# Three small edits in a four-layer graph network on one core: two seed copies, small vector instructions, the last store

## The chip, the cores and the metric

The kernel runs on one core of a Trainium2 chip. A core has a matrix engine (PE, with its weight loads shown as PEld), a vector engine (DVE), an activation engine (ACT), a general engine (POOL) and a queue engine (SP); each takes its instructions in order. Matrix products land in PSUM, which has eight banks. Data moves between the main memory and the on-chip memory by 16 DMA engines; transfers are started by instructions in the queue of SP or POOL. The metric is the device time of one execution in microseconds (us), lower is better.

## The reference

The input is a feature matrix x of 3327 x 128 and a sparse symmetric weight matrix adj of 3327 x 3327. Each of four layers adds to x a function of h = relu(layernorm(x)):

```python
# layer 0: attention; 128 "heads" of width 8, the scores of all share adj twice as a bias
a = softmax(einsum('dnh,dmh->dnm', q, k) * 128 ** -0.5 + adj + adj, axis=2)
x = x + einsum('dnm,dmh->dnh', a, v).reshape(n, h * d) @ Wo.T
# layer 1: hyperbolic: h_mul(x, W) = exp_map(log_map(x) @ W), h_add = Moebius addition
h1 = h_add(h_mul(h, embed), embed_bias)
neigh = exp_map_zero(adj @ log_map_zero(h1))
x = x + h_add(h_mul(concatenate((h, neigh), axis=1), layer), layer_bias)
# layer 2: hyperbolic again, with projections into a ball, and relu between two maps
# layer 3: x + (adj / deg) @ h @ W_in + (adj.T / deg_T) @ h @ W_out
```

The maps of the hyperbolic layers scale each row by a number made of norms, tanh and artanh. All is float32.

## The kernel before, in words

**Order.** A first part (L313 to L423) projects q, k and v and writes them to main memory, in halves that PE can take in a faster form. An upper bound for the scores is worked out so that no maximum is needed. Then comes the attention loop (L512 to L747), then the output projection of layer 0 (L804 to L838), then layers 1, 2 and 3 (from L969 on). An older, slower form of the attention stands behind a branch and does not run here.

**The attention loop.** The 3327 query columns are cut into 7 chunks of 476 (the last one 472). The 128 heads are taken four at a time (32 groups, g), and the 3328 keys as 13 pairs of 128-row tiles (q). A unit u is one (chunk, group, pair): 7 x 32 x 13 = 2912 units. For a unit there are two rows of work, r = 0 and 1, each with its own PSUM bank in one of three buffers S[u % 3]. S[0] has three banks, of which a unit uses bank 1 and one of the others in turn (`banks`, L595); S[1] and S[2] have two.

The work of one unit: DVE seeds each of the two banks with a tile of adj, less the bound (`seed`, L620, copy in L623). For each of the four heads j, PE adds a product that turns the scores of head j - 1 into those of head j (`scores`, L625, L629), and ACT takes the exponential of both banks in one instruction into tile e (`exps`, L636, L641). For j = 3 in S[1] and S[2] the exponential is split into two halves, one for each bank, so that the first bank comes free earlier. Then PE multiplies the exponentials of all four heads by the values into one bank po (`values`, L644, L649). After 13 pairs DVE copies po away (L661) and POOL stores it (L665).

The order of the instructions is written out by hand: the loop at L723 runs over slots i, four for a unit, and lists at each slot which unit's exponential, seed, scores and values come next. For u % 3 = 0 the two seeds stand in two different slots (at = 0 and 2). For the others both stand at slot at = 1, one directly after the other. Between slots, DVE also transposes squares of adj for a later chunk (L275, L279).

**Waits.** A framework puts a semaphore wait wherever two instructions touch the same tile. Banks of one tile count as the same tile. `touch` (L606) therefore keeps, for each of the three buffers, the last twelve accesses, and tells the framework of pairs on other banks that they need not wait; of accesses to the same bank it adds the wait by hand. Before the change it does so only for instructions of two different engines, so the second seed of a pair waits, on DVE, for the first.

**The layers.** Rows of x lie as 128 partitions x 26 tiles (row = 26 p + t, so partition 127 holds 25 rows), in the tile xs. A number for each row is a 128 x 26 tile; the class `Small` (L137) has helpers for such tiles, each of which issues one instruction of 26 columns on DVE, or on ACT for a function: `tt` (L147, record at L149), `ts` (L158, L161 and L163), `recip` (L166), `act` (L174, L176), and made of these `sqrt` (L179, ACT's root with one refining step) and `artanh` (L185). `artanh` works out both a series for small arguments and a logarithm for the others and picks by a mask. `ball_sum` (L965) and `sum_norm` (L975) work out the two factors of a Moebius sum and its norm. In this part the framework's scheduler, and not the program's order, places the instructions.

The root is called 16 times (once in the first part, once at L784, once in each of three layer norms, six times in layer 1, five times in layer 2), artanh six times, `ball_sum` three times and `sum_norm` twice. In each layer `aggregate` (L930) loads 26 strips of adj or its transpose, by turns on POOL and SP, and PE multiplies them (L941); DVE sums the strips of some layers (L944).

**The end.** After the last aggregation, seven chunks of four row tiles each (the last has two) are projected (L1095), added into xs by DVE (L928), and stored: partitions 0 to 126 by SP (L1113) and partition 127, which has one row fewer, by POOL (L1115). Where the strips have 127 rows the helper `pieces` (L68) cuts them into 112 and 15.

Of the kernel before, what the change touches and what calls it, by code (L numbers as in the profile page):

```python
# [9 lines left out]

F32 = mybir.dt.float32


# [3 lines left out]
AF = mybir.ActivationFunctionType  # L17
ALU = mybir.AluOpType
# [4 lines left out]
P = 128  # L23
# [4 lines left out]
NT = 26  # L28
# [39 lines left out]
def pieces(m):  # L68

    return [(0, 112), (112, m)] if m == P - 1 else [(0, m)]  # L70
# [13 lines left out]
def gnn_kernel(ctx: ExitStack, tc: tile.TileContext, x, adj, Wq, Wk, Wv, Wo, embed, layer,  # L84
               embed_bias, layer_bias, weight, bias, W_in, W_out, out):
    nc = tc.nc
    dram = ctx.enter_context(tc.tile_pool(name="dram", bufs=1, space=DRAM))
    const = ctx.enter_context(tc.tile_pool(name="const", bufs=1))

    ident = const.tile([P, P], F32, name="ident")  # L90
    make_identity(nc, ident)

    adjT = dram.tile([NP, NP], F32, name="adjT")
    by_tile = adjT.rearrange("(p t) n -> t p n", t=NT)
    v_d = dram.tile([NP, HD], F32, name="v_d")
    n2_d = {s: dram.tile([GP], F32, name=f"n2{s}_d") for s in "qk"}
    kraw_d = dram.tile([H, GP], F32, name="kraw_d")

    qS_d = dram.tile([2, H, GP], F32, name="qS_d")
    kS_d = dram.tile([2, H, HEADS, NP], F32, name="kS_d")  # L100
# [36 lines left out]
    class Small:  # L137
# [33 lines left out]
        def div(self, a, b):  # L171
            return self.mul(a, self.recip(b))

        def act(self, a, f):  # L174
            o = self.new()
            nc.scalar.activation(o, a, f)  # L176
            return o

        def sqrt(self, a):  # L179

            v = self.ts(a, 1e-30, ALU.max)
            s = self.act(v, AF.Sqrt)
            return self.ts(self.add(s, self.div(v, s)), 0.5, ALU.mult)

        def artanh(self, a, top):  # L185

            v = self.ts(a, top, ALU.min)
            v2 = self.mul(v, v)
            s = self.ts(v2, 1.0 / 13.0, ALU.mult, 1.0 / 11.0, ALU.add)
            for k in (9.0, 7.0, 5.0, 3.0, 1.0):  # L190
                s = self.ts(self.mul(s, v2), 1.0 / k, ALU.add)
            s = self.mul(s, v)
            r = self.div(self.ts(v, 1.0, ALU.add), self.ts(v, -1.0, ALU.mult, 1.0, ALU.add))
            g = self.ts(self.act(r, AF.Ln), 0.5, ALU.mult)
            small = self.ts(v, 0.25, ALU.is_lt)
            return self.add(g, self.mul(small, self.tt(s, g, ALU.subtract)))

    def sumsq(sm, a, tmp):
        nc.scalar.activation(tmp, a, AF.Square)
# [113 lines left out]
    with tc.tile_pool(name="a1", bufs=1) as a1, tc.tile_pool(name="a2", bufs=2) as a2, \  # L313
# [3 lines left out]
        xs = load_x(a1)  # L317
# [19 lines left out]
        for t0 in range(0, NT, 2):  # L337
            for s in "kq":
                st = {i: a2.tile([P, H, 2 * P], F32R if s == "q" else F32, name=f"st_{s}{i}")
                      for i in range(2 if s == "q" else 1)}  # L340
                n2 = a2.tile([P, 2, P], F32, name=f"n2{s}")
                for i in range(2):
                    t = t0 + i
# [83 lines left out]
    with tc.tile_pool(name="d1", bufs=1) as d1, tc.tile_pool(name="d2", bufs=2) as d2, \  # L427
# [17 lines left out]
        with tc.If(loose > 0):  # L445
# [28 lines left out]
            for c in range(NC):  # L474
# [5 lines left out]
                with tc.For_i(0, HEADS, 1) as d:  # L480
# [12 lines left out]
                    for t in range(NT):  # L493
                        m = rows_of(t)
                        s = d_ps.tile([P, 4 * P], F32, name="ps_y")
# [16 lines left out]
    with tc.tile_pool(name="e1", bufs=1) as e1, tc.tile_pool(name="e_adj", bufs=30) as e_adj, \  # L512
# [7 lines left out]
        VA = [e1.tile([P, NT, 4, H + 1], F32, name=f"VA{i}") for i in range(2)]  # L520

        seen = e1.tile([P, 3], F32, name="seen")
        S = [e_ps.tile([P, 3 if i == 0 else 2, 512], F32, name=f"S{i}") for i in range(3)]
        po = e_ps.tile([P, 512], F32, name="po")

# [54 lines left out]
        with tc.If(loose < 1), tc.manual_schedule():  # L580
# [25 lines left out]
            def touch(u, rows, x):  # L606
                of = {banks(u)[r] for r in rows}
                for y, other in touched[u % 3]:
                    if not of & other and x.ins.engine != y.ins.engine:
                        tc.declare_no_dep(x.ins, y.ins, reason="other banks")  # L610
                for i in of:
                    if (u % 3, i) in last:
                        tc.add_manual_dep(x.ins, last[u % 3, i].ins.name, after, reason="the same bank")
                    last[u % 3, i] = x
                touched[u % 3].append((x, of))

            def bank(u, r):
                return S[u % 3][:, banks(u)[r], :width_of(pairs[u][0])]

            def seed(u, r):  # L620
                c, g, q = pairs[u]
                w = width_of(c)
                touch(u, [r], nc.vector.tensor_copy(bank(u, r), adj_of[c][2 * q + r][:, :w]))  # L623
# [99 lines left out]
            for i in range(-4, 4 * n + 15):  # L723
                u, j = in_slot(i)
                if 0 <= u < n:
                    exps(u, j)

                u, at = (i + 4) // 4, i % 4
                if u < n and (u % 3 == 0 and at in (0, 2) or u % 3 and at == 1):
                    for r in range(2) if at == 1 else (at // 2,):  # L730
                        seed(u, r)
                u = (i - 14) // 4
                if at == 2 and 0 <= u < n and pairs[u][2] == NQ - 1:
                    store(u)
                if at == 3 and i > 0:
                    for f, a in behind.pop(i // 4, ()):
                        f(*a)
                if at % 2:
                    for k in (1, 2):
                        u, j = in_slot(i + k)  # L740
                        if 0 <= u < n:
                            scores(u, j)
                    u, r = ((i - 11) // 4, 0) if at == 3 else ((i - 13) // 4, 1)
                    if 0 <= u < n:
                        values(u, r)
                if at == 0 and 0 <= i // 4 < n:
                    loads(i // 4)  # L747


    xs = load_x(const)  # L750
# [28 lines left out]
    eb2, lb2, b2 = row_sum("eb2", eb), row_sum("lb2", lb), row_sum("b2", hb)  # L779
    with tc.tile_pool(name="w0", bufs=1) as w0:  # L780
        sm = Small(w0, "s")
# [183 lines left out]
    def ball_sum(sm, coef, aa, ab, y2, least):  # L965

        xy = sm.mul(coef, ab)
        x2 = sm.mul(sm.mul(coef, coef), aa)
        e = sm.ts(xy, 2.0, ALU.mult, 1.0, ALU.add)  # L969
        na = sm.ts(e, y2[:, 0:1], ALU.add)  # L970
        den = sm.ts(sm.add(e, sm.ts(x2, y2[:, 0:1], ALU.mult)), least, ALU.max)
        rd = sm.recip(den)
        return sm.mul(sm.mul(na, coef), rd), sm.mul(sm.ts(x2, -1.0, ALU.mult, 1.0, ALU.add), rd)

    def sum_norm(sm, al, be, aa, ab, y2):  # L975

        b2 = sm.ts(sm.mul(be, be), y2[:, 0:1], ALU.mult)
        n2 = sm.add(sm.mul(sm.mul(al, al), aa), b2)
        return sm.sqrt(sm.add(n2, sm.mul(sm.ts(sm.mul(al, be), 2.0, ALU.mult), ab)))


    with tc.tile_pool(name="g1", bufs=1) as g1:
        sm = Small(g1, "s")
# [5 lines left out]
        a, aa = arr("a", D + 1), sm.new()  # L989
# [9 lines left out]
        ab = a[:, :, D]  # L999
        al, be = ball_sum(sm, c1, aa, ab, eb2, L1_EPS)  # L1000
        yn = sm.ts(sum_norm(sm, al, be, aa, ab, eb2), L1_EPS, ALU.max)
        f = sm.div(sm.artanh(yn, L1_MAX_TANH), yn)
        al, be = sm.mul(al, f), sm.mul(be, f)
        y = arr("y")
# [25 lines left out]
        al, be = ball_sum(sm, c2, ww, w1[:, :, D], lb2, L1_EPS)  # L1030
# [5 lines left out]
    with tc.tile_pool(name="h1", bufs=1) as h1:  # L1036
        sm = Small(h1, "s")
# [3 lines left out]
        a, aa = arr("a", D + 1), sm.new()  # L1041
# [4 lines left out]
        ab = a[:, :, D]  # L1046
        al, be = ball_sum(sm, c1, aa, ab, hb2, L2_MIN_NORM)
# [3 lines left out]
        f = sm.mul(sm.div(sm.artanh(pn, L2_MAX_TANH), pn), pf)  # L1051
        al, be = sm.mul(al, f), sm.mul(be, f)
        y = arr("y")
# [6 lines left out]
        u, rr = arr("y"), sm.new()  # L1060
        for c in range(7):
            ts = tiles_of(c)
# [9 lines left out]
        n2 = sm.ts(sm.mul(t1, p2), L2_MIN_NORM, ALU.max)  # L1072
# [8 lines left out]
    with tc.tile_pool(name="i1", bufs=1) as i1:  # L1081
        sm = Small(i1, "s")
        h = arr("h")
        layer_norm(sm, xs, h)
        deg = sm.new()
        nc.vector.memset(deg, 1.0)

        def over_degree(g):
            pos = sm.ts(g, 0.0, ALU.is_gt)
            return sm.recip(sm.add(sm.mul(g, pos), sm.ts(pos, -1.0, ALU.mult, 1.0, ALU.add)))  # L1090

        def add_projected(c, ps, lhsT, w, r):
            ts = tiles_of(c)
            for t in ts:
                nc.tensor.matmul(ps[:, (t - ts[0]) * P:(t - ts[0] + 1) * P], lhsT[:, t * P:(t + 1) * P], w,  # L1095
                                 start=True, stop=True)
            for t in ts:
                add_scaled(xs[:, t, :], ps[:, (t - ts[0]) * P:(t - ts[0] + 1) * P], r[:, t:t + 1], xs[:, t, :])

        r_out = over_degree(degT)  # L1100
        pu, width = aggregate(h, strip_rows, deg)
        vT = matT("hT")
        by_tiles(pu, width, vT)
        r_in = over_degree(deg)
        pu, width = aggregate(h, strip_T, also={
            3 * c + 4: lambda c=c: add_projected(c, bank_u(7), vT, w_out, r_out) for c in range(7)})
        uT = matT("uT")
        by_tiles(pu, width, uT)
        for c in range(7):
            add_projected(c, next_bank(), uT, w_in, r_in)  # L1110
            ts = tiles_of(c)
            m = ts[-1] + 1 if ts[-1] < NT - 1 else NT - 1
            nc.sync.dma_start(out[0:(P - 1) * NT].rearrange("(p t) d -> p t d", t=NT)[:, ts[0]:ts[-1] + 1, :],  # L1113
                              xs[0:P - 1, ts[0]:ts[-1] + 1, :])
            nc.gpsimd.dma_start(out[(P - 1) * NT + ts[0]:(P - 1) * NT + m].rearrange("(p t) d -> p t d", p=1),  # L1115
                                xs[P - 1:P, ts[0]:m, :])

# [29 lines left out]
```

## Time and profile before

| what | value |
|---|---|
| runs | 11603.74 us median of 3 (11602.49 to 11605.68) |
| the profiled execution, its own time | 11601.16 us |
| its span, first to last instruction | 11599.4 us |
| busy in the span | PE 95%, ACT 90%, DVE 41%, PEld 30%, POOL 16% |
| mean granted PE clock | 0.976 |
| attention loop, first to last exponential | 456.2 to 10572.3 us |
| layers 1 to 3 with the last stores | about 10680 to 11599 us |

The profile is one execution taken by the hardware profiler. For each group of instructions it gives the source line, the engine, the operation, the tiles as out<-in with their shapes, how often it ran, the busy time in all, the mean length of one in ns, and the time that the engine stood idle just before them with what ended most of it. The records of ACT and DVE run from the start of an instruction to the end of its writes, and those of neighbours overlap. The chain that ended last follows the work back from the last instruction to what released it. A helper's line (L149, L161, L928) stands for all that call it.

### The profile page before, as it was taken

Reading aid. Unit: us, or ns where it says so; the run is one execution under the profiler, and the core shown is the slowest. Engines: PE = TensorE matmul, PEld = TensorE weight load, DVE = VectorE, ACT = ScalarE, POOL = GpSimd, SP = SyncE. Lnnn points to the kernel's source line nnn. Section 1 sums busy time; section 2 is a strip of 40 time slices with the busy share of each in tenths; the row PEclk is TensorE's granted clock in tenths of the full one; section 3 lists DMA queues with packets and bytes.
Section 4 is the critical chain, followed back from the end, with each engine's and each line's share of the span. In section 5 each row is a group of like instructions: output and inputs, shape, how many; then the busy total and the mean of one; then the engine's idle time right before and its main releaser. Section 6 shows DMA issues by size and latency. Waiting matters only on the chain.

```text
span 11599.4 us, 196522 instructions
## 1 busy us (share of the span) xinstructions
PE 10982.6 (95%) x72980; PEld 3500.4 (30%) x72980; DVE 4766.2 (41%) x7583; ACT 10411.4 (90%) x14091; POOL 1895.5 (16%) x3254
## 2 busy tenths in 40 slices
PE   4699999999999999999999999999999999998787
PEld 2122222222222222222222222222222222224443
DVE  5344444444444443444444444444443333335631
ACT  3699999999999999999999999999999999995210
POOL 5211112111121111211112111121111211110000
PEclk8799999999999999999999999999999999998888
DMA  8755455554555554555555545555454544443465
GB/s 247 245 90 93 86 93 105 90 92 88 94 103 91 91 88 83 102 93 90 89 92 103 93 89 92 90 105 93 87 92 78 103 81 79 82 78 103 153 230 211
DMA packets 652389, 1242.80 MB, mean 107 GB/s; under 512 B 185742, under 2 KB 527766, under 8 KB 634924
## 3 DMA queue, kind: packets, MB, share of 16 engines
q1 hardware_dynamic: 609768, 1100.81, 48.6%
q0 software_dynamic: 41664, 129.31, 3.7%
q8 instruction: 590, 9.67, 0.4%
q14 instruction: 367, 3.01, 0.1%
HBM read 1082.90 MB, written 146.60 MB: 106 GB/s over the span
## 4 chain that ended last, share of the span: by engine, by line
ACT 80%; PE 8%; issue 6%; DVE 2%; DMA 1%; POOL 0%; SPq 0%; DVEq 0%; POOLq 0%; ACTq 0%
ACT e L641 79%; PE pu L941 5%; PE S L629 1%; PE po L649 1%; DVE S L623 0%; PE pu L893 0%; DMA ot<-oT_d 0%; PE ps_y L837 0%; DVE xs L928 0%; PE pu L916 0%; PE pu L904 0%; POOL a L571 0%; DVE s L149 0%; DMA KT<-kS_d 0%; DVE s L944 0%
## 5 line engine op out<-in xcount | busy, mean ns | idle before, releaser
L641 ACT ACTIVATE e<-S 128x952 f32<-128x952 f32 (+3 forms) x13589 | 10107.1, 914 | 9.0 <-PE S L629 7.7
L623 DVE COPY S<-a 128x476 f32<-128x476 f32 (+1 forms) x5824 | 3739.6, 655 | 5991.9 <-ACT e L641 5731.8
L649 PE MATMUL po<-e,VA 128*9 128x476 f32 (+1 forms) x46592 | 5736.9, 564 | 16.1 <-DVE OS L661 3.1
L629 PE MATMUL S<-QS,KT 64*128 64x476 f32 (+1 forms) x23296 | 5077.6, 442 | 112.2 <-DVE S L623 30.0
L629 PEld LDWEIGHTS S<-QS,KT 64*128 64x128 f32 x23296 | 2273.0, 184 | 5383.0 <-DVE S L623 2705.4
L665 POOL DMA_DIRECT2D oT_d<-OS x896 | 470.7, 531 | 5604.3 <-DVE OS L661 5468.5
L649 PEld LDWEIGHTS po<-e,VA 128*9 128x9 f32 x46592 | 691.2, 88 | 1793.5 <-issue 1694.1
L550 POOL TENSOR_SCALAR QS<-QS 32x476 fp32r<-32x476 f32 (+1 forms) x1344 | 784.7, 584 | 1334.2 <-DMA QS<-qS_d 748.0
L123 ACT COPY uT<-pu 128x494 f32<-128x494 f32 (+1 forms) x12 | 6.6, 547 | 428.6 <-PE pu L941 428.6
L560 POOL COPY VA<-VR 128x832 f32<-128x832 f32 x224 | 198.6, 886 | 951.7 <-DMA VR<-v_d 729.6
L941 PE MATMUL pu<-strip,h 128*128 128x494 f32 (+2 forms) x728 | 293.9, 564 | 40.3 <-ACT h L874 40.3
L941 PE MATMUL pu<-strip,y 128*128 128x494 f32 (+2 forms) x728 | 296.8, 570 | 34.4 <-DVE y L928 19.9
L571 POOL TENSOR_TENSOR a<-a,shb 128x476 f32<-128x476 f32 (+1 forms) x182 | 213.3, 1207 | 245.1 <-DMA a<-adjT 221.3
L275 DVE STREAM_TRANSPOSE cols<-rows 128x416 f32<-128x416 f32 x208 | 203.2, 982 | 21.4 <-DMA rows<-in_adj_dram 14.1
L941 PEld LDWEIGHTS pu<-strip,y 128*128 128x128 f32 (+1 forms) x728 | 139.9, 193 | 190.5 <-issue 157.8
L941 PEld LDWEIGHTS pu<-strip,h 128*128 128x128 f32 (+1 forms) x728 | 138.0, 191 | 192.3 <-issue 141.5
L661 DVE COPY OS<-po 128x476 f32<-128x476 f32 (+1 forms) x224 | 145.6, 650 | 53.2 <-PE po L649 47.2
L123 ACT COPY hT<-pu 128x494 f32<-128x494 f32 (+1 forms) x4 | 2.2, 549 | 136.2 <-PE pu L941 136.2
L407 ACT CAST st_k<-st_q 128x1664 fp32r<-128x1664 f32 x16 | 53.7, 3378 | 75.9 <-DMA st_q<-kraw_d 58.0
L939 POOL DMA_DIRECT2D strip<-adjT x39 | 20.9, 535 | 600.7 <-PE pu L941 598.9
L944 DVE TENSOR_REDUCE s<-strip 128x1 f32<-128x3327 f32 (+1 forms) x26 | 93.9, 3616 | 59.7 <-DMA strip<-in_adj_dram 59.7
L944 DVE TENSOR_REDUCE degT<-strip 128x1 f32<-128x3327 f32 (+1 forms) x26 | 94.0, 3616 | 54.0 <-DMA strip<-adjT 54.0
(173 smaller groups left out, 1714.9 us busy)
## 6 DMA issues: line engine op xcount, KB each, us to landing
KT<-kS_d SPq DMA_DIRECT2D x1792, 208.0 KB
KT<-kS_d SPq DMA_DIRECT2D x1792, 104.0 KB
VR<-v_d SPq DMA_DIRECT2D x224, 416.0 KB
strip<-adjT POOLq DMA_DIRECT2D x39, 1663.5 KB, 7.7
strip<-adjT SPq DMA_DIRECT2D x36, 1663.5 KB
QS<-qS_d SPq DMA_DIRECT2D x3072, 14.9 KB
QS<-qS_d SPq DMA_DIRECT2D x1536, 29.8 KB
adjT<-cols SPq DMA_DIRECT2D x26, 1664.0 KB
```

The lines of the kernel that those rows point to most:

```text
L275: nc.vector.transpose(self.cols[:, t0:t0 + NQ, 32 * j:32 * j + 32], self.rows.rearrange("p (x t) -> p t x", t=NT)[:, t0:t0 + NQ, :])
L550: nc.gpsimd.tensor_scalar(QS[b][r0:r0 + 32, j + 1, :w], QS[b][r0:r0 + 32, j, :w].bitcast(F32), -1.0, 0.0, op0=ALU.mult, op1=ALU.add)
L560: nc.gpsimd.tensor_copy(VA[(c * NG + g) % 2][:, :, :, 0:H], v.rearrange("p j (t e) -> p t j e", e=H))
L571: nc.gpsimd.tensor_tensor(a[:, :w], a[:, :w], shift[:, :w], op=ALU.subtract)
L623: touch(u, [r], nc.vector.tensor_copy(bank(u, r), adj_of[c][2 * q + r][:, :w]))
L629: x = nc.tensor.matmul(bank(u, r), KT[b][64 * r:64 * r + 64, max(0, j - 1), q * P:(q + 1) * P], QS[b][64 * r:64 * r + 64, j, :w], start=Fa ...
L641: touch(u, range(a, b), nc.scalar.activation(e[:, a:b, :w], S[u % 3][:, lo + a:lo + b, :w], AF.Exp, scale=2.0))
L649: nc.tensor.matmul(po[32 * j:32 * j + H + 1, :w], VA[k % 2][:, 2 * q + r, j, :], e_of[u, j][:, at, :w], start=(q == 0 and r == 0), stop=(q ...
L661: nc.vector.tensor_copy(o[:, :w], po[:, :w])
L665: nc.gpsimd.dma_start(oT_d[:, d * N + c * CW:d * N + c * CW + w], o[32 * j:32 * j + H + 1, :w])
L941: nc.tensor.matmul(pu[c][:, :w], y[:m, t, :], s[:m, c * AW:c * AW + w], start=(t == 0), stop=(t == NT - 1))
L944: nc.vector.tensor_reduce(deg[:m, t:t + 1], s[:m], axis=AX.X, op=ALU.add)
```

## The change

There are three edits.

1. In `touch`, an access of DVE to S[1] or S[2] is no longer made to wait for an earlier access of DVE to another bank. Between the two seeds of such a unit, DVE now writes a zero into a tile of one element, `apart`.
2. The small tiles use a fused instruction, (a op0 scalar) op1 b, where two stood before. `sqrt` lets ACT take the root of v / 4 and folds the halving into the fused step. `artanh` takes the logarithm ahead of the series, and the series has one fused step for each coefficient instead of two. `ball_sum` and `sum_norm` are regrouped in the same way.
3. The last store cuts partitions 0 to 126 into 112 on SP and 15 on POOL.

```diff
+        def fused(self, a, s, op0, b, op1):
+            o = self.new()
+            nc.vector.scalar_tensor_tensor(o, a, s, b, op0=op0, op1=op1)
+            return o
         def sqrt(self, a):
             v = self.ts(a, 1e-30, ALU.max)
-            s = self.act(v, AF.Sqrt)
-            return self.ts(self.add(s, self.div(v, s)), 0.5, ALU.mult)
+            s = self.act(v, AF.Sqrt, 0.25)
+            return self.fused(self.div(v, s), 0.25, ALU.mult, s, ALU.add)
         def artanh(self, a, top):
             v = self.ts(a, top, ALU.min)
             v2 = self.mul(v, v)
-            s = self.ts(v2, 1.0 / 13.0, ALU.mult, 1.0 / 11.0, ALU.add)
-            for k in (9.0, 7.0, 5.0, 3.0, 1.0):
-                s = self.ts(self.mul(s, v2), 1.0 / k, ALU.add)
-            s = self.mul(s, v)
-            r = self.div(self.ts(v, 1.0, ALU.add), self.ts(v, -1.0, ALU.mult, 1.0, ALU.add))
-            g = self.ts(self.act(r, AF.Ln), 0.5, ALU.mult)
+            r = self.fused(v, 1.0, ALU.add, self.recip(self.ts(v, -1.0, ALU.mult, 1.0, ALU.add)), ALU.mult)
+            g = self.act(r, AF.Ln)
+            s = self.ts(v2, 1.0 / 13.0, ALU.mult)
+            for k in (11.0, 9.0, 7.0, 5.0, 3.0):
+                s = self.fused(s, 1.0 / k, ALU.add, v2, ALU.mult)
+            s = self.fused(s, 1.0, ALU.add, v, ALU.mult)
             small = self.ts(v, 0.25, ALU.is_lt)
-            return self.add(g, self.mul(small, self.tt(s, g, ALU.subtract)))
+            d = self.fused(g, -0.5, ALU.mult, s, ALU.add)
+            return self.fused(g, 0.5, ALU.mult, self.mul(small, d), ALU.add)
...
+        apart = e1.tile([1, 1], F32, name="apart")
...
                 for y, other in touched[u % 3]:
-                    if not of & other and x.ins.engine != y.ins.engine:
+                    if not of & other and (x.ins.engine != y.ins.engine or u % 3 and x.ins.engine == DVE):
                         tc.declare_no_dep(x.ins, y.ins, reason="other banks")
...
                     for r in range(2) if at == 1 else (at // 2,):
                         seed(u, r)
+                        if at == 1 and r == 0:
+                            nc.vector.memset(apart, 0.0)
...
         e = sm.ts(xy, 2.0, ALU.mult, 1.0, ALU.add)
-        na = sm.ts(e, y2[:, 0:1], ALU.add)
-        den = sm.ts(sm.add(e, sm.ts(x2, y2[:, 0:1], ALU.mult)), least, ALU.max)
-        rd = sm.recip(den)
-        return sm.mul(sm.mul(na, coef), rd), sm.mul(sm.ts(x2, -1.0, ALU.mult, 1.0, ALU.add), rd)
+        rd = sm.recip(sm.ts(sm.fused(x2, y2[:, 0:1], ALU.mult, e, ALU.add), least, ALU.max))
+        na = sm.fused(e, y2[:, 0:1], ALU.add, coef, ALU.mult)
+        return sm.mul(na, rd), sm.mul(sm.ts(x2, -1.0, ALU.mult, 1.0, ALU.add), rd)
...
-        b2 = sm.ts(sm.mul(be, be), y2[:, 0:1], ALU.mult)
-        n2 = sm.add(sm.mul(sm.mul(al, al), aa), b2)
-        return sm.sqrt(sm.add(n2, sm.mul(sm.ts(sm.mul(al, be), 2.0, ALU.mult), ab)))
+        b2 = sm.fused(be, y2[:, 0:1], ALU.mult, be, ALU.mult)
+        cross = sm.mul(sm.fused(al, 2.0, ALU.mult, be, ALU.mult), ab)
+        return sm.sqrt(sm.add(sm.mul(sm.mul(al, aa), al), sm.add(b2, cross)))
...
-            nc.sync.dma_start(out[0:(P - 1) * NT].rearrange("(p t) d -> p t d", t=NT)[:, ts[0]:ts[-1] + 1, :],
-                              xs[0:P - 1, ts[0]:ts[-1] + 1, :])
+            for p0, p1 in pieces(P - 1):
+                (nc.gpsimd if p0 else nc.sync).dma_start(
+                    out[p0 * NT:p1 * NT].rearrange("(p t) d -> p t d", t=NT)[:, ts[0]:ts[-1] + 1, :],
+                    xs[p0:p1, ts[0]:ts[-1] + 1, :])
             nc.gpsimd.dma_start(out[(P - 1) * NT + ts[0]:(P - 1) * NT + m].rearrange("(p t) d -> p t d", p=1),
                                 xs[P - 1:P, ts[0]:m, :])
```

More of the change, by code (lines that the diff above doesn't have):

```diff
@@ L9 @@
 from concourse.masks import make_identity
+DVE = mybir.EngineType.DVE
 F32 = mybir.dt.float32
@@ L172, in div, with act @@
             return self.mul(a, self.recip(b))
-        def act(self, a, f):
+        def act(self, a, f, scale=1.0):
             o = self.new()
-            nc.scalar.activation(o, a, f)
+            nc.scalar.activation(o, a, f, scale=scale)
+            return o
+        def fused(self, a, s, op0, b, op1):
+            o = self.new()
+            nc.vector.scalar_tensor_tensor(o, a, s, b, op0=op0, op1=op1)
             return o
```

## The prediction

> **What bounds the kernel now.** I read the share of each engine first, then the chain that ended last, then the groups of the attention loop, then the records inside one stretch of it, and last the tail. From the page of before: the busy shares, the chain, and three groups (busy time, mean ns of one, then the engine's idle time before them).
>
> ```profile
> PE 10982.6 (95%) x72980; PEld 3500.4 (30%) x72980; DVE 4766.2 (41%) x7583; ACT 10411.4 (90%) x14091; POOL 1895.5 (16%) x3254
> ...
> ACT 80%; PE 8%; issue 6%; DVE 2%; DMA 1%; POOL 0%; SPq 0%; DVEq 0%; POOLq 0%; ACTq 0%
> ...
> L641 ACT ACTIVATE e<-S 128x952 f32<-128x952 f32 (+3 forms) x13589 | 10107.1, 914 | 9.0 <-PE S L629 7.7
> L623 DVE COPY S<-a 128x476 f32<-128x476 f32 (+1 forms) x5824 | 3739.6, 655 | 5991.9 <-ACT e L641 5731.8
> L629 PE MATMUL S<-QS,KT 64*128 64x476 f32 (+1 forms) x23296 | 5077.6, 442 | 112.2 <-DVE S L623 30.0
> ```
>
> The exponentials of L641 fill 10107 us of 11599 with 9 us idle before them. But each record (mean 0.914 us) overlaps its neighbour, so a busy ACT might still be a waiting one. I therefore took starts and ends of single records. In the stretch from 5016 us, ends lie 0.855 to 0.859 us apart for a 952-column tile and 0.460 for a 476-column one, whatever the starts do: one start came 0.942 after the one before it instead of the usual 0.845, and its end came 0.855 after. Over the loop the median distance of ends is 0.857 (8320 tiles of 952), 0.460 (3328 of 476), 0.850 (1387 of 944) and 0.457 (554 of 472). The product is 7130 + 1531 + 1179 + 253 = 10093 us; from first start to last end the loop takes 10116. **ACT is the limit, and only some 23 us of the loop are not its own work.** In 227 places the ends lie more than 20 ns too far apart, 26 us in sum (a few other distances are shorter than the median): this is all that a faster feed can win there.
>
> Second, the end. The timeline of the tail (start, length, engine, what):
>
> ```profile
> 11528.14 6.81 DVE L928 SCALAR_TENSOR_TENSOR xs<-pu,s,xs 128x128 f32<-128x128 f32 x26 [1.25 <-PE pu L1095]
> 11529.29 55.20 SPq L1113 DMA_DIRECT2D out_dram<-xs  x7
> 11529.56 0.52 POOL L1115 DMA_DIRECT2D out_dram<-xs  x1 [30.93 <-DVE xs L928]
> ...
> 11534.72 0.98 POOL L1115 DMA_DIRECT2D out_dram<-xs  x2 [0.55 <-DVE xs L928]
> ```
>
> Compute is over at 11535, yet SP issues stores until 11584.5 and the span ends at 11599.4. The view by stretches sets this beside a stretch in which a 112-row strip piece arrives (the last two columns: share of 16 DMA engines, GB/s):
>
> ```profile
> 11504.00:11510.00 6.00, 6.00 (x19) 3.10 (x18) 0.55 (x2) 0.00 (x0) 0.00 (x0) 1.00 0.94 251
> 11535.00:11598.00 63.00, 0.00 (x0) 0.00 (x0) 0.00 (x0) 0.00 (x0) 0.69 (x2) 0.50 0.07 25
> ```
>
> A share of 0.07 of 16 is about one engine. The 127-row store goes through a single one at 25 GB/s; the 112 + 15 rows of the last strip used 0.94 of all.
>
> **The change, part by part.** *The store* (L1113). 762 packets of 2 KB (median 84 ns) and 127 of 1 KB (46 ns) are now drained one after another. With 112 rows over 16 engines a chunk is 7 packets in a row, 7 x 0.084 = 0.6 us, less than the 1.03 us in which DVE makes a chunk, so SP no longer backs up. What is late next is POOL: it issues 14 stores instead of 7, each 0.49 us (the "0.98 x2" row), so 0.98 per chunk against 1.03: it just keeps up. After DVE's end at 11534.95 come 0.3 us to the first issue, two issues (1.0), landing 4.6 to 5.9 us counted from the start of the last issue, so 11535.7 + 5.9 = 11541.6, and 1.15 us of closing steps (from SP's last store wait at 11598.25 to the end): 11543. Bounds: 11541 with the short landing and nothing queued, 11549 if POOL's issues take twice as long and a 15-row piece sits on one engine (15 x 0.084 = 1.3 us). **Term: 11599.4 - 11543 = -56.4** (-50 to -58).
>
> *The two seeds of a pair* (L623, for u % 3 in 1, 2). Two rows of the loop, starts and lengths:
>
> ```profile
> 5006.41 1.42 DVE L623 COPY S<-a 128x476 f32<-128x476 f32 x2 [1.48 <-ACT e L641]
> ...
> 5009.90 1.97 DVE L623 COPY S<-a 128x476 f32<-128x476 f32 x3 [1.16 <-ACT e L641]
> ```
>
> A pair takes 1.42, so the second starts 0.76 after the first. The third of three, which has no wait on DVE, adds only 0.55. In the records, 752 copies without a wait follow a copy by 0.566, and 24 whose wait on POOL was already met do so too, so a met wait costs nothing. The self-wait goes (0.76 - 0.566 = 0.194), the 1x1 memset comes in; the nearest row is a memset of 128x1, after which DVE starts its next instruction 0.08 later:
>
> ```profile
> 10699.52 0.06 DVE L952 MEMSET uT<- 128x1 f32 x1
> 10699.60 0.29 DVE L869 BATCH_NORM_STATS2 st<-xs 128x6 f32<-128x128 f32 x1
> ```
>
> So the second copy comes 0.194 - 0.08 = 0.114 us earlier. Its own wait for the second half of the exponential is met by then: the half ends 0.46 after the first half, the copy starts 0.65 after the first copy. PE, which waits for it, gains the same; DVE, at 41%, hides 1941 memsets x 0.08 = 155 us. ACT gains only where it ran dry. Taking at most 0.114 off each of the 227 places gives 17 us. In 53 of them (2.8 us) the second copy is seen to be the last event; in most of the others PE is late behind a pair and a row of waits for loads, so it would be earlier too, but not everywhere by all of it. **Term: -12** (0 to -20).
>
> By the Trainium skill, "VectorE: DVE Perf Modes", section "The DRAIN you can't avoid", eight copies take as long with a semaphore after each as with one at the end. By that this term would be 0. The 0.76 against 0.566 above disagrees; the rule stays as a rival.
>
> *Small instructions.* A square root loses one DVE instruction, artanh 7 (23 to 16), the ball sum 2 (13 to 11), the norm of a sum 2 beside its root: 16 + 42 + 6 + 4 = 68. Their worth depends on what stands beside them. A chain in which each needs the one before costs 0.217 a step, as here in the series of artanh:
>
> ```profile
> 10754.06 0.19 DVE L149 TENSOR_TENSOR s<-s,s 128x26 f32<-128x26 f32 x1
> 10754.28 0.18 DVE L161 TENSOR_SCALAR s<-s 128x26 f32<-128x26 f32 x1
> 10754.49 0.19 DVE L149 TENSOR_TENSOR s<-s,s 128x26 f32<-128x26 f32 x1
> 10754.71 0.18 DVE L161 TENSOR_SCALAR s<-s 128x26 f32<-128x26 f32 x1
> ```
>
> With independent work between, a step costs 0.09. Exposed series (PE waits behind them, 10751 to 10758, 11001 to 11005, 11012 to 11017, 11190 to 11196): 4 x 5 steps x 0.217 = 4.3. Two more artanh lie in stretches where DVE is full: 2 x 7 x 0.09 = 1.3. Nine exposed roots: 2.0. Five sums, 2 each at about 0.15: 1.5. Against it stands the fused form: at 128x128 its rows show 0.344 against 0.284 for a plain product, so it may cost up to 0.06 more; at 26 columns I take a fifth of it on 40 exposed ones, 0.5. The earlier logarithm buys little, since its table load is already beside the series. Sum -8.6. Bounds: -4 (fused form at full price, 2.4, and half of the interleaved steps hidden) to -15, because ahead of the last layer four 3.6 us sums of strips stand within the chain of the norm, and one step less may move one of them out or in. **Term: -8.6.**
>
> **Sum.** -56.4 - 12 - 8.6 = -77. The profiled execution took 11601.16 (span 11599.4), 2.6 below the median 11603.74. From 11601.2 that is 11524; with half of the distance to the median, **11526**.
>
> **The rivals.**
> 1. *The self-wait is free, or nothing that ACT waits for hangs on it.* For: 26 us in all, 2.8 seen directly. Against: 0.76 to 0.566. Then -56.4 - 8.6: 11536. Chance 0.20.
> 2. *The starts are ACT's true pace.* Starts lie 0.845 apart at best, and twice in three tiles' turn (10.41 us) one comes later, 0.942 and 0.884: 0.136 us x 970 turns = 132 us would be won, 11404. Against: the even ends. Chance 0.05.
> 3. *The store stays at one engine's speed* (two queues in place of one, same engines). Then only -20.6: 11581. Against: 0.94 of the engines at 112 rows. Chance 0.05. The Trainium skill, "DMA: Bandwidth & Descriptors", section "Rules for kernel authors", says that spreading DMAs over issuing engines gives no bandwidth; by that alone this case would hold, were the row count not changed as well.
> 4. *Slower: the memset is no filler but a second link.* If it waits for the first copy and the second copy for it, the spacing becomes 0.76 + 0.06 + 0.10 = 0.92, 0.16 later than now. In the stretch read, ACT has 0.04 us in hand after a late pair (records of 1.00 against 0.964 where it ran dry), so 0.12 is lost per pair: 1941 x 0.12 = 233 us, 11769. It decides from a spacing of 0.80 on and eats the other terms at 0.80 + 65/1941 = 0.833. Against: the memset writes a tile that no copy touches. Chance 0.06.
>
> **How the numbers follow.** Forecast 0.64 (11526), rivals 0.20, 0.05, 0.05, 0.06. The range takes the forecast with its bounds and the first rival: low 11526 - 20, high 11536 + 8: 11506 to 11544. Rivals 2 to 4 and a little of the others lie outside. A measurement tells 0.2% (23 us) from no change: faster 0.89 (forecast, rivals 1 and 2), same 0.05 (rival 3), slower 0.06.
>
> **What would show it.** Store: SP's seven issues within 8 us instead of 55, the span's end within 9 us of the last DVE instruction. Pair: two copies with the memset in 1.30 us instead of 1.42, ends of the exponentials still 0.857 apart, L641's total unchanged, L629's idle and the 227 places fewer. Layers: 68 DVE instructions fewer beside 1941 memsets, series at five steps. It would be wrong if ends move closer than 0.857 (rival 2), the pair grows beyond 1.46 (rival 4), or SP still issues long after DVE is done.

## The result and the profile after

The changed kernel takes 11513.02 us (median of 4 runs, 11505.02 to 11513.99) against 11603.58 (4 runs) for the kernel before in the same comparison: a ratio of 0.992, 95% interval 0.9903 to 0.9937. The profiled execution took 11513.99 us, its span is 11512.2. Between the two spans lie 87.2 us.

The page of the kernel after: busy shares, the chain that ended last, and the same groups as before (lines have moved: L650 is the exponential, L632 the seed, L638 the scores).

```profile
PE 11042.9 (96%) x72980; PEld 3752.1 (33%) x72980; DVE 4640.8 (40%) x9456; ACT 10396.0 (90%) x14091; POOL 1895.0 (16%) x3261
...
ACT e L650 59%; PE po L658 13%; PE S L638 12%; PE pu L952 5%; PE pu L904 0%; PE ps_y L848 0%; PE pu L927 0%; DVE OS L670 0%; DVE xs L939 0%; DMA ot<-oT_d 0%; PE pu L915 0%; DVE s L955 0%; DMA KT<-kS_d 0%; PE ps_t L844 0%; DVE s L935 0%
...
L650 ACT ACTIVATE e<-S 128x952 f32<-128x952 f32 (+3 forms) x13589 | 10091.6, 1067 | 4.0 <-PE S L638 3.7
L632 DVE COPY S<-a 128x476 f32<-128x476 f32 (+1 forms) x5824 | 3620.0, 660 | 6100.6 <-ACT e L650 6052.3
L638 PE MATMUL S<-QS,KT 64*128 64x476 f32 (+1 forms) x23296 | 5147.0, 446 | 24.9 <-DVE S L632 20.2
```

PE's idle time before the scores fell from 112.2 us to 24.9; 30.0 and 20.2 of these are put down to a seed, in 42 and 3 waits. The exponential's mean record grew from 0.914 to 1.067 us although its total fell: the record begins earlier, with the scores lying ready, and its end still lies 0.857 after the one before. So a longer record here means less waiting. DVE has 1873 instructions more: 1941 memsets less 68.

Both spans, divided at the same events, show where the 87.2 us went:

| stretch (us) | before | after | difference |
|---|---|---|---|
| start to first exponential | 456.2 | 456.8 | +0.5 |
| attention loop | 10116.0 | 10095.6 | -20.4 |
| loop's end to the first aggregation | 185.8 | 183.8 | -2.0 |
| between aggregations, after layer 1's and after layer 2's | 111.1 + 61.7 | 107.1 + 60.3 | -5.4 |
| the aggregations of layers 1, 2 and 3 | 148.4 + 148.4 + 298.5 | 148.2 + 146.9 + 298.4 | -1.8 |
| from the last aggregation product to the end (the tail) | 73.2 | 15.1 | -58.1 |

Layer 3 has two aggregations, one behind the other without a gap. In the loop the median distances of the exponentials' ends are the same as before (857, 460, 850, 457 ns). Places where they lie over 20 ns too far apart (late places) fell from 227 (25.9 us) to 14 (5.3 us).

The timeline of DVE in the loop after (start, length, engine, what):

```profile
5017.43 1.26 DVE L632 COPY S<-a 128x476 f32<-128x476 f32 x2 [2.37 <-ACT e L650]
5018.07 0.06 DVE L742 MEMSET apart<- 1x1 f32 x1
```

A pair takes 1.26 us instead of 1.42. Its ends lie 0.599 apart (median) instead of 0.760.

The tail after, and the view by stretches of its last 12 us (the last two columns: share of 16 DMA engines, GB/s):

```profile
11499.09 6.81 DVE L939 SCALAR_TENSOR_TENSOR xs<-pu,s,xs 128x128 f32<-128x128 f32 x26 [1.25 <-PE pu L1105]
11500.25 6.00 SPq L1124 DMA_DIRECT2D out_dram<-xs  x7
11500.51 0.53 POOL L1124 DMA_DIRECT2D out_dram<-xs  x1 [30.93 <-DVE xs L939]
11501.03 0.53 POOL L1127 DMA_DIRECT2D out_dram<-xs  x1
...
11507.44 0.50 POOL L1127 DMA_DIRECT2D out_dram<-xs  x1
```

```profile
11500.00:11506.00 6.00, 3.97 (x36) 3.77 (x34) 5.90 (x23) 0.00 (x0) 5.18 (x11) 1.00 0.59 181
11506.00:11512.00 6.00, 0.00 (x0) 0.00 (x0) 0.00 (x0) 0.00 (x0) 1.94 (x4) 0.53 0.34 107
```

SP issues its seven stores in 6.0 us, in step with DVE. The DMA engines are 0.59 busy while DVE still works; before, 0.08 then and 0.07 after it had ended. The span ends 6.3 us after DVE's last instruction.

### The profile page after: what moved, and what is told of

It is laid out like the page before. It is cut to its first block, busy times and chain, and to the rows that moved or that the text cites. A ratio compares the mean times of both kernels' runs of the same rounds, so it can differ in the third digit from the quotient of the medians.

```text
span 11512.2 us, 196520 instructions
## 1 busy us (share of the span) xinstructions
PE 11042.9 (96%) x72980; PEld 3752.1 (33%) x72980; DVE 4640.8 (40%) x9456; ACT 10396.0 (90%) x14091; POOL 1895.0 (16%) x3261
## 4 chain that ended last, share of the span: by engine, by line
ACT 59%; PE 31%; issue 4%; DVE 1%; DMA 0%; POOL 0%; SPq 0%; POOLq 0%; DVEq 0%; ACTq 0%
ACT e L650 59%; PE po L658 13%; PE S L638 12%; PE pu L952 5%; PE pu L904 0%; PE ps_y L848 0%; PE pu L927 0%; DVE OS L670 0%; DVE xs L939 0%; DMA ot<-oT_d 0%; PE pu L915 0%; DVE s L955 0%; DMA KT<-kS_d 0%; PE ps_t L844 0%; DVE s L935 0%
## 5 line engine op out<-in xcount | busy, mean ns | idle before, releaser
L650 ACT ACTIVATE e<-S 128x952 f32<-128x952 f32 (+3 forms) x13589 | 10091.6, 1067 | 4.0 <-PE S L638 3.7
L632 DVE COPY S<-a 128x476 f32<-128x476 f32 (+1 forms) x5824 | 3620.0, 660 | 6100.6 <-ACT e L650 6052.3
L658 PE MATMUL po<-e,VA 128*9 128x476 f32 (+1 forms) x46592 | 5737.2, 564 | 15.7 <-DVE OS L670 4.3
L638 PE MATMUL S<-QS,KT 64*128 64x476 f32 (+1 forms) x23296 | 5147.0, 446 | 24.9 <-DVE S L632 20.2
L638 PEld LDWEIGHTS S<-QS,KT 64*128 64x128 f32 x23296 | 2530.0, 183 | 5254.9 <-ACT e L650 2390.7
L340 PE MATMUL ps_t<-wk,hT 128*128 128x512 f32 x104 | 58.8, 700 | 60.8 <-ACT sq L362 60.8
## 6 DMA issues: line engine op xcount, KB each, us to landing
QS<-qS_d SPq DMA_DIRECT2D x1536, 29.8 KB
```

The lines of the kernel that those rows point to most:

```text
L638: x = nc.tensor.matmul(bank(u, r), KT[b][64 * r:64 * r + 64, max(0, j - 1), q * P:(q + 1) * P], QS[b][64 * r:64 * r + 64, j, :w], start=Fa ...
L650: touch(u, range(a, b), nc.scalar.activation(e[:, a:b, :w], S[u % 3][:, lo + a:lo + b, :w], AF.Exp, scale=2.0))
L658: nc.tensor.matmul(po[32 * j:32 * j + H + 1, :w], VA[k % 2][:, 2 * q + r, j, :], e_of[u, j][:, at, :w], start=(q == 0 and r == 0), stop=(q ...
```

## The experiments

Ten kernels. The three single edits and the store with both pieces on SP ran beside one median of the kernel before (11607.7), the cuts at 126 and 113 rows beside another (11599.7), the other four beside a third (11599.8); ratios are against these.

**One edit alone.** Three kernels, each the kernel before with one part of the change.

*The pair alone*:

```diff
-                    if not of & other and x.ins.engine != y.ins.engine:
+                    if not of & other and (x.ins.engine != y.ins.engine or u % 3 and x.ins.engine == DVE):
...
+                        if at == 1 and r == 0:
+                            nc.vector.memset(apart, 0.0)
```

> The kernel before with the first edit alone: no wait between the two seeds of a pair, the memset between them. Theory (ACT is the limit of the attention loop and can win only where it ran dry; in the trace of the changed kernel such places fell from 227 to 14): the loop from first start to last end goes from 10116 to 10096 us, distances of the exponentials' ends stay at 0.857 and 0.460, and the time goes from 11603.6 to 11583. Rival (the loop's 20 us come from elsewhere, a wait on DVE costs nothing): 11603. Rival (the pair is worth more by itself, the other edits hide some of it): below 11575.

Measured: 11587.3, ratio 0.9982 (0.9973 to 0.9991), 20.4 us. The pair's ends lie 0.598 apart, 12 late places are left of the 227; tail and gaps are those of before. The loop took 10103.2 in this execution, 7.6 more than in the kernel after, and no wait accounts for it: the distances of full tiles (952 columns) average 857.7 ns instead of 857.1, all shifted together. So ACT's own pace differs between executions whose loops hold the same instructions; why, no run here shows.

*The store alone*:

```diff
-            nc.sync.dma_start(out[0:(P - 1) * NT].rearrange("(p t) d -> p t d", t=NT)[:, ts[0]:ts[-1] + 1, :],
-                              xs[0:P - 1, ts[0]:ts[-1] + 1, :])
+            for p0, p1 in pieces(P - 1):
+                (nc.gpsimd if p0 else nc.sync).dma_start(
...
```

> The kernel before with the last edit alone: the store of partitions 0 to 126 cut into 112 on SP and 15 on POOL. Theory (the 127-row store used one DMA engine, and this is all that the tail waited for): 58 us less, 11545.5; the end of the span comes 15 us after the last product of an aggregation instead of 73. Rival (part of the shorter tail is due to the shorter chains before it): more than 11550.

Measured: 11548.17, ratio 0.9949 (0.9935 to 0.9962), 59.5 us. Tail 15.5 instead of 73.2; the loop (10115.4, 227 places) is untouched.

*The small instructions alone* (the helpers, `ball_sum` and `sum_norm` as in the change; its core):

```diff
-            for k in (9.0, 7.0, 5.0, 3.0, 1.0):
-                s = self.ts(self.mul(s, v2), 1.0 / k, ALU.add)
+            for k in (11.0, 9.0, 7.0, 5.0, 3.0):
+                s = self.fused(s, 1.0 / k, ALU.add, v2, ALU.mult)
```

> The kernel before with the second edit alone: fewer small instructions. Theory (worth what stands between the aggregations, taken from the two traces: 2.0 + 4.0 + 1.4 us between them and 1.7 us in them): 9 us less, 11594.5. Rival (the instructions were hidden, and the gaps got shorter because the strips came earlier): no change, 11603. The three edits alone should add up to the 87 us between the two traces; if they do not, they help or hinder one another.

Measured: 11597.62, ratio 0.9991 (0.9982 to 1.0), 10.1 us, by the runs alone not told from no change. Its profile shows where it lies: the gaps take 182.9, 108.4 and 60.3 (7.0 less than before), two aggregations 146.9 and 147.3 (2.6 less); loop (10116.0, 227 places) and tail (73.2) as before. Aggregations between 146.9 and 148.5 come up in kernels that share these instructions too, so the 2.6 are not surely the edit's.

The three medians add up to 20.4 + 59.5 + 10.1 = 90.0; all together gave 90.6 (11603.58 - 11513.02). Each edit changed its own stretch of the profile alone, so they do not touch one another. The intervals, 10 us or more to each side, are far wider than the 0.6 between the two sums; that these agree so closely is luck.

**Why the store was slow.** The prediction said: 127 rows go through one DMA engine, 112 and 15 are shared out. Four kernels ask which of it matters: the rows, the second queue, or the queue that issues.

*Both pieces on SP*:

```diff
-                (nc.gpsimd if p0 else nc.sync).dma_start(
+                nc.sync.dma_start(
```

> The changed kernel with both pieces of the store, 112 and 15 rows, on SP's queue. Theory (the row count matters, not the second queue): the end stays within 2 us of the changed kernel's 15 us after the last aggregation, 11511 to 11514; it may come 1 us earlier since POOL has seven stores fewer. Rival (the second queue is what made the tail short): SP backs up again and the end comes 10 us or more later, above 11523.

Measured: 11518.92, ratio 0.9923 (0.9909 to 0.9936). The tail takes 14.7, no longer than with two queues; the 6 us against the kernel after lie mostly in the loop (10102.6, 9 late places, full tiles at 857.6 ns), ACT's pace again. The kernel before, too, was 4.1 us slower beside this run than beside the kernel after. The second queue is worth nothing here.

*127 rows whole, but on POOL*:

```diff
-            for p0, p1 in pieces(P - 1):
-                (nc.gpsimd if p0 else nc.sync).dma_start(
...
+            nc.gpsimd.dma_start(out[0:(P - 1) * NT].rearrange("(p t) d -> p t d", t=NT)[:, ts[0]:ts[-1] + 1, :],
+                              xs[0:P - 1, ts[0]:ts[-1] + 1, :])
```

> The kernel after, but the 127-row store of a chunk stays whole and is issued by POOL instead of SP. Theory (the row count decides: 127 rows have no even share over 16 engines, so they go through one at 25 GB/s, whatever queue issues them): the tail is as long as before, 73 us after the last aggregation product instead of 15, so about 11513 + 58 = 11571 (11560 to 11580). Rival (what cost the 58 us is SP's way of issuing, or its being behind with the strips, and POOL cuts transfers otherwise): tail 15 to 20 us, 11513 to 11520.

Measured: 11510.81, ratio 0.9923 (0.9907 to 0.994), tail 15.2. My theory fell, the rival held. The DMA view of the last stretch and the view by stretches:

```profile
out_dram<-xs POOLq DMA_DIRECT2D x6, 254.0 KB, 3.2
```

```profile
11502.00:11508.00 6.00, 2.00 (x18) 1.81 (x17) 3.93 (x16) 0.00 (x0) 5.77 (x12) 0.89 0.78 226
```

A whole 254 KB store lands 3.2 us after its issue, and the engines are 0.78 busy at 226 GB/s. In the list of packets the same rows stand as 409 of 4 KB and a few odd sizes, where SP's queue had 762 of 2 KB and 127 of 1 KB. So the queue that issues decides too: POOL's shares out 127 rows, SP's does not.

*The cut elsewhere: 126 + 1 and 113 + 14*:

```diff
-            for p0, p1 in pieces(P - 1):
+            for p0, p1 in ((0, 126), (126, P - 1)):
```

> The kernel after, with the 127 rows of a chunk's store cut into 126 on SP and 1 on POOL. Theory (SP's queue shares the rows of a transfer among as many engines as divide the row count, up to 16: 127 rows went to 1, 112 to 16, 15 to 15): 126 rows go to 14 engines, a chunk drains in 9 x 4 packets of 0.084 us, about 3 us at worst, tail 15 to 20 us, 11513 to 11520. Rival (only a multiple of 16 rows is shared out): 126 rows through one engine, tail about 72 us, 11570.

Measured: 11514.69, ratio 0.9926 (0.9909 to 0.9943), tail 15.7.

```diff
-            for p0, p1 in pieces(P - 1):
+            for p0, p1 in ((0, 113), (113, P - 1)):
```

> The kernel after, with the cut one row further: 113 on SP and 14 on POOL. Theory (the divisor of the row count decides, and 113 is a prime): 678 packets of 2 KB and 113 of 1 KB one after another, 678 x 0.084 + 113 x 0.046 = 62 us instead of the 70 of 127 rows, tail 73 - 8 = 65, 11563 (11555 to 11570). Rival (two pieces are enough, or SP's rest beyond 112 goes to another engine): tail 15 to 25, 11513 to 11523.

Measured: 11562.92, ratio 0.9968 (0.9956 to 0.9981), tail 66.6 where 65 was worked out. SP's seven issues, one after another, and the stretch after DVE's end:

```profile
11497.05 48.84 SPq L1124 DMA_DIRECT2D out_dram<-xs  x7
```

```profile
11506.00:11550.00 44.00, 0.00 (x0) 0.00 (x0) 0.00 (x0) 0.00 (x0) 1.20 (x3) 0.50 0.07 27
```

48.84 us and a share of 0.07: the picture of before, with one row more than 112. Two pieces alone do not help, and 126 rows, no multiple of 16, do. The trace agrees with a count of engines: on SP's queue each engine that takes part in a transfer closes it with a packet of 4 bytes, and for seven stores there are 7 of these with 127 rows, 112 with 112, 105 with 15, 98 with 126, and 7 with 113, so 1, 16, 15, 14 and 1 engines. The times of the packets say the same without that reading: with 127 and with 113 rows one packet of rows ran at a time, at some moments two; with 112 and 126 rows up to 18 overlapped.

By the Trainium skill, "DMA: Bandwidth & Descriptors", section "Why a DMA increments its semaphore by 16 and not by 1", a transfer is shared among the largest number up to 16 that divides its rows, except that some copies issued by POOL are shared among 16 whatever their rows. All five row counts on SP and the 127 rows on POOL bear this out.

**What a pair may cost.** Two kernels with the second copy later.

*The memset kept, the wait kept too*:

```diff
-                    if not of & other and (x.ins.engine != y.ins.engine or u % 3 and x.ins.engine == DVE):
+                    if not of & other and x.ins.engine != y.ins.engine:
```

> The kernel after with its 1x1 memset between the two copies of a pair, but the second copy still made to wait for the first. Theory (the wait is what costs; the memset only takes its own issue time): ends of the two copies 0.76 us apart with the memset hidden beneath the wait, or up to 0.81 with its 0.045 on top; the loop falls back to 10116 with some 230 dry places (11533), or, since only about 0.04 us per pair were in hand, to 10120 to 10160 (11537 to 11575). Rival (an instruction in between gives the first copy the time that the wait would take, so that the wait costs nothing): 0.60 apart, loop 10096, 11513.

Measured: 11529.63, ratio 0.994 (0.9924 to 0.9957). Ends 0.760 apart, 221 late places (22.8 us), loop 10113.0. Of the loop's gain 17 of 20 us are lost again, and the memset adds nothing while there is a wait to hide beneath. The second copy starts 0.76 after the first, and PE's and ACT's rows are back at those of before:

```profile
5017.02 0.66 DVE L632 COPY S<-a 128x476 f32<-128x476 f32 x1 [2.07 <-ACT e L650]
5017.66 0.06 DVE L742 MEMSET apart<- 1x1 f32 x1
5017.78 1.21 DVE L632 COPY S<-a 128x476 f32<-128x476 f32 x2
```

```profile
L650 ACT ACTIVATE e<-S 128x952 f32<-128x952 f32 (+3 forms) x13589 | 10105.9, 914 | 7.1 <-PE S L638 5.9
...
L638 PE MATMUL S<-QS,KT 64*128 64x476 f32 (+1 forms) x23296 | 5077.0, 442 | 111.5 <-DVE S L632 29.8
```

Is it the wait that costs, or the instruction that carries it? The wait for the first copy stands in DVE's queue as a semaphore instruction of its own, and with the wait most of these are gone. The view of the seed's line has them (how many; shortest, median and longest in ns), before and after:

```profile
L623 DVEq EVENT_SEMAPHORE  x2973: 21/21/3927, 426.5 to 10563.8; - x199
```

```profile
L632 DVEq EVENT_SEMAPHORE  x1090: 21/21/3936, 426.1 to 10538.2; - x182
```

Before, it starts 0.039 us after the first copy's end, takes 0.021, and the second copy starts 0.044 later: 0.657 + 0.039 + 0.021 + 0.044 is the 0.76. In the kernel after, 58 pairs still have such an instruction between their copies, for a wait on ACT that was already met, and their ends lie 0.599 apart like the others'. So the instruction by itself costs nothing; having to come after the first copy's end does.

*A longer memset*:

```diff
-        apart = e1.tile([1, 1], F32, name="apart")
+        apart = e1.tile([1, 256], F32, name="apart")
```

> The kernel after with a memset of 1x256 in place of 1x1, some 0.27 us longer. Theory (the exponentials now wait about 0.2 us more in ACT's queue than before, 0.04 + 0.16 in hand per pair, and a later second copy goes through to ACT beyond that): ends of the copies 0.60 + 0.27 = 0.87 apart, 0.07 short per pair, 1941 x 0.07 = 136 us, 11649 (11600 to 11690). Rival (PE is no direct link, pairs have more in hand than the records show): loop 10096 to 10116, 11513 to 11533.

Measured: 11629.53, ratio 1.0025 (1.0016 to 1.0035): slower than before, with the store's gain in it. Ends 0.856 apart, loop 10211.1, 115.5 more than after. The exponentials are late in 2019 places, by a median of 53 ns, about once a pair. So a pair that is (0.856 - 0.599) = 0.257 later is 0.053 too late: in the kernel after, the second copy can come 0.204 us later before an exponential waits for it, and in the kernel before it could come 0.204 - 0.161 = 0.043 later. DVE's timeline, and the group of the scores:

```profile
5016.17 0.66 DVE L632 COPY S<-a 128x476 f32<-128x476 f32 x1 [2.37 <-ACT e L650]
5016.85 0.27 DVE L742 MEMSET apart<- 1x256 f32 x1
5017.06 0.62 DVE L632 COPY S<-a 128x476 f32<-128x476 f32 x1
```

```profile
L638 PE MATMUL S<-QS,KT 64*128 64x476 f32 (+1 forms) x23296 | 5102.7, 442 | 188.8 <-DVE S L632 172.2
```

Here the memset stands between the copies, and PE idles 188.8 us, nearly all of it for a seed.

**Is ACT the limit?** Narrower exponentials, PE's work unchanged in size:

```diff
-                    touch(u, range(a, b), nc.scalar.activation(e[:, a:b, :w], S[u % 3][:, lo + a:lo + b, :w],
+                    touch(u, range(a, b), nc.scalar.activation(e[:, a:b, :w - 28], S[u % 3][:, lo + a:lo + b, :w - 28],
...
-                                     e_of[u, j][:, at, :w], start=(q == 0 and r == 0),
+                                     e_of[u, j][:, at, :w // 2].unsqueeze(1).to_broadcast([P, 2, w // 2]), start=(q == 0 and r == 0),
```

> The kernel after, with the exponentials of each bank 28 columns narrower; the products with the values read the first half of the tile twice, so PE's work keeps its size, and the output leaves out half of the columns. Theory (ACT alone is the limit, PE has room): at 0.834 ns an element a full tile ends 46.7 ns earlier, a half 23.4: 9707 x 46.7 + 3882 x 23.4 = 544 us, 10969. Rival (PE is right behind ACT): PE was busy 989 of 1000 us before and 998 now by its overlapping records; if that is its true load, the loop loses under 100 us, 11413 to 11513. A time between the two would say how much room PE has.

Measured: 11001.88, ratio 0.9484 (0.9468 to 0.95). The loop takes 9585.2, 510 of the 544 us less. Ends lie 810 and 437 ns apart (857 and 460 before), as 0.834 ns a column has it (56 columns less are 47 ns); the missing 34 us are 241 late places (38.4). PE's products with the values took 5739.5 us in all, 5737.2 in the kernel after, so that work did keep its size. ACT is the limit with at least 5% of room on PE behind it (510 of 10096 us), and PE's busy share never showed that room:

```profile
PE 10521.4 (96%) x72980; PEld 3388.2 (31%) x72980; DVE 4645.3 (42%) x9456; ACT 9872.8 (90%) x14091; POOL 1894.6 (17%) x3261
...
PE 89%; ACT 3%; DVE 2%; issue 1%; DMA 1%; POOL 0%; SPq 0%; POOLq 0%; DVEq 0%; ACTq 0%
```

The chain names PE for 89% here, though the ends still keep ACT's pace to the nanosecond. So the chain's share did not tell here which of two engines side by side sets the pace; the distances of ends did.

## Why the prediction came out as it did, point by point

- **What bounds it: right.** The ends stayed 0.857 apart, and narrowing ACT alone moved them. The 26 us of late places were all that there was to win.
- **The store: right in size (-58.1 for -56.4), in part by luck, and incomplete in its cause.** SP's seven issues within 8 us: 6.0. The span's end within 9 us of DVE: 6.3. POOL "just keeps up" held: its 14 issues of 0.51 us run on 2.0 us after DVE. The last lands 2.1 us after its start, where I had taken 4.6 to 5.9 from before. Those long landings came up only beside a store that drains through one engine: with 113 rows on SP they are back, 4.8 to 6.3. What then ends the span is POOL's closing step, 11507.2 to 11511.4, which the sum did not have. From DVE's end to the last issue's start, its landing and the closing the sum took 0.8 + 5.9 + 1.15; the trace has 1.5 + 2.1 + 2.7. So a landing much too long stood against an issue and a closing too short. The step "127 rows go through a single engine" is true of SP's queue alone.
- **The pair: right in sign and mechanism, low in size (-20.4 for -12, just beyond its bound of -20).** Two terms were off. The memset was priced at 0.08 from a memset ahead of another kind of instruction; between two copies it costs 0.599 - 0.555 = 0.044 by ends (0.555 is the distance of copies with nothing between, in the kernel before). So the copy comes 0.161 earlier, not 0.114: that alone lifts the sum over the late places from 17.4 to 19.5. And I took 5 off for places that would not gain fully; nearly all did, the eight of 0.18 us and more that remain being mostly at the loop's first and last units.
- **Small instructions: -8.6 expected; -9.6 by the pieces of that kernel's profile alone (7.0 of it in the gaps), -9.2 by the table above (2.0 + 5.4 + 1.8).** 68 fewer as counted. The fused form, for which 0.5 was charged, repeats every 0.220 in a chain, against 0.217 for a plain step: it costs next to nothing.
- **The sum.** -77 expected, -87 between the spans; 11526 against 11513.02.
- **Rival 1 (the self-wait is free)** fell: with the wait put back, all of the loop's gain but 3 us goes. What the Trainium skill, "VectorE: DVE Perf Modes", section "The DRAIN you can't avoid", measured for its eight copies, that a semaphore after each costs nothing extra, does not hold for these: 0.760 with the wait, 0.555 without.
- **Rival 2 (starts are ACT's pace)** fell by the even ends. **Rival 3 (two queues, same engines)** fell by the share of 0.59, though its premise was sound: two queues alone give nothing.
- **Rival 4 (a second link)** did not come about, but its price list was tested by the longer memset. It put the point from which a pair decides at 0.80 and the break-even at 0.833. Measured by ends: 0.599 + 0.204 = 0.803. The longer memset stands at 0.856 and is 29.8 us (0.25%) slower than before, which puts the break-even at 0.856 - 29.8 / 1941 = 0.841.

## What to carry to other kernels

Read a queue-fed engine's pace from the distances of its ends. Here the starts lay closer together than the ends for most tiles, the busy shares put PE (95%) ahead of ACT (90%), and the chain of waits named ACT before and PE in the narrowed kernel, though ACT set the pace in both. The late places among the ends are the whole of what a faster feed could win. A wait for the instruction just ahead on the same engine is not free (0.2 us here); before anything is put into or taken out of a step, know how much later the step could come without harm. When a large store trails behind finished compute, look at the share of DMA engines in that stretch first: the row count, by its divisors, and the queue that issues decide how many take part.

## What the runs showed that was not expected

- POOL's queue shares out a store of 127 rows that SP's queue puts through one engine (tail 15.2 against 73.2), in packets of 4 KB (0.159 us) instead of 2 KB (0.084).
- The record of the 1x1 memset begins at 5018.07, after the second copy's start: that copy starts 0.574 after the first (median), at about 5018.00. In the program the memset stands ahead of that copy, so records of neighbours on DVE need not show their order.
- An exponential costs 63 ns and 0.834 ns a column: (857 - 460) / 476 = 0.834, and 857 - 952 x 0.834 = 63. The narrowed tiles, not used for this, fit: 63 + 896 x 0.834 = 810.
- ACT's pace differs by 0.6 ns per full tile between executions with the same loop (857.1 and 857.7 on average, with almost no late places in either), 7 us over the loop. That is nearly as much as the whole edit of the small instructions.
